# A four-layer graph attention network: the columns W a of layers l = 1 to 3 computed on TensorE from W turned

## The chip, the cores and the metric

The kernel runs on one core of a Trainium2 chip, in one launch. The time is the device time of one execution in microseconds (us); the median of three executions is compared. Engines are named as in the profile: PE is TensorE (PEld its weight loads), DVE is VectorE, ACT is ScalarE, POOL is GpSimd, SP is SyncE, which only issues DMAs here.

## The reference

The input x has 16 batch elements of 1024 nodes with 256 features, and one adjacency matrix of 1024 x 1024 serves all. Four layers follow each other; each normalises the rows of x, applies ReLU, and adds the result of a graph attention layer to x. Cut to one layer with H heads of D = 256 / H features (H is 4, 1, 4, 1 for l = 0 to 3; the slope is 0.2, 0.2, 0.2, 0.01):

```
h = max(layernorm(x), 0)
q = (h @ W).reshape(B, N, H, D)
e_src = einsum('bnhd,hd->bnh', q, a_src);  e_dst = einsum('bnhd,hd->bnh', q, a_dst)
e = leaky_relu(e_src[:, :, None, :] + e_dst[:, None, :, :], slope)
attn = softmax(where(mask, e, -inf), axis=2)
x = x + act(einsum('bijh,bjhd->bihd', attn, q))        # elu, relu in the last layer
```

Layer 0 has one pair of vectors a for all heads, layer 2 one pair for each head, layers 1 and 3 have one head. Since e_src = h (W a_src), the kernel appends W a_src and W a_dst to W as extra columns and gets the scores out of the projection itself. How these columns of W a are computed is what the change touches; it is done once per layer, for all batch elements.

## The kernel before, in words

Four batch elements (streams) are under way at once. The order of the 64 steps (one step is one layer of one batch element) is fixed by `order_of_steps`: streams 0, 1, 2, 0, 3, 1, 2, and so on. The program is written in the order in which each engine is to work; semaphores are put in by the framework, and a tile of a pool with n buffers waits until the one n allocations ago has been read for the last time.

*A step.* The preparation of a step (lines 231 to 376) takes the statistics of the rows on DVE (`stats`, L243), combines them on POOL or DVE, normalises on ACT (L290), turns the rows (by TensorE, L321, in the first two steps and the last; else by ACT L299, a transposing DMA L301 and ACT L307), projects on TensorE (`project`, L332, with W and its appended columns in `wx[l]`) and copies the result with ACT (L334). From the appended columns come the factors `rcol` (L340) and `gcol` (L350, L351); `gcol` is turned into rows (L358, L360), written to DRAM (`grow`, L362) and fetched back, spread over all partitions (`gs`, L386), and ACT copies it to PSUM as `g` (L397). For each head and each of the eight blocks of nodes, DVE makes one tile of attention weights `w` (L411, one instruction on 128 x 1024), and TensorE multiplies it with the projected rows (`aggregate`, L428); ACT copies the sums to `y` (L443). `finish` divides, applies the activation and adds to x on DVE, ACT and POOL.

*Order.* A step has eight groups of aggregation. After group k of step n the loop at lines 673 to 696 runs, in this order: pieces of the finish of the step before, one piece out of the dictionary `later` if position 8 n + k has one (L690), the pieces of coming preparations that are due at this position (`prepare`), and new `w` tiles (`emit_tiles`). `w` has WBUFS = 18 buffers, also used for other tiles of that name; PSUM has four buffers named `bank`.

*The columns.* `weight_columns(l)` gives four pieces: `vectors` fetches the two vectors (2 KB) into partition 0 of a `w` tile (L145, one DMA), `spread` copies them to all partitions with one matmul against ones (L152) and ACT (L155), `columns` multiplies W with them on DVE and sums each head (L162 and L163, four times each) and squares (L169), `bound` sums the squares over the partitions on TensorE (L175), takes the maximum on DVE (L178) and makes three bias values on POOL (L179 to L182). For l = 0 this runs at the very beginning. For l = 1, 2, 3 the pieces stand at positions 1, 27 and 43 of `later` and 1, 2 and 8 positions after (L670).

At the start SP issues, in this order: x of stream 0, W of l = 0, the eight blocks of the adjacency matrix, x of stream 1, W of l = 1, x of streams 2 and 3 (L631 to L638). W of l = 2 and 3 follows at L668.

Of the kernel before, what the change touches and what calls it, by code (L numbers as in the profile page):

```python
# [26 lines left out]
F32 = mybir.dt.float32  # L27
# [4 lines left out]
AF = mybir.ActivationFunctionType  # L32
ALU = mybir.AluOpType
# [3 lines left out]
P = 128  # L37
# [3 lines left out]
WBUFS = 18  # L41
# [29 lines left out]
def kernel(ctx: ExitStack, tc: tile.TileContext, x, adj, ws, avs, out):  # L71
    nc = tc.nc
    B, N, F = x.shape
    C = N // P
    K = F // P
    HALF = C // 2

    const = ctx.enter_context(tc.tile_pool(name="const", bufs=1))

    ident = const.tile([P, P], F32, name="ident")  # L80
# [10 lines left out]
    wx = []  # L91
# [12 lines left out]
    small = ctx.enter_context(tc.tile_pool(name="small", bufs=4))  # L104
    work = ctx.enter_context(tc.tile_pool(name="work", bufs=2))
# [5 lines left out]
    L = len(LAYERS)  # L111
# [4 lines left out]
    def bank(*shape):  # L116
        t = ps.tile([P, 512], F32, name="bank")
        n = math.prod(shape)
        if len(shape) == 1:
            return t[:, 0:n]  # L120
        names = "abc"[:len(shape)]
        return t[:, 0:n].rearrange(f"p ({' '.join(names)}) -> p {' '.join(names)}",
                                   **dict(zip(names, shape)))

    def heads_of(t, H):


        return t[..., 0:F + H].rearrange("p c (h d) -> p c h d", h=H)

    def load_weights(l, queue=nc.sync):  # L130
        H = LAYERS[l][0]
        for k in range(K):
            queue.dma_start(out=heads_of(wx[l], H)[:, k, :, 0:F // H],
                            in_=ws[l][k * P:(k + 1) * P, :].rearrange("p (h d) -> p h d", h=H))

    def weight_columns(l):

        H, slope, hs, _ = LAYERS[l]
        D = F // H
        st = {}  # L140

        def vectors(queue=nc.sync):

            st["a"] = work.tile([P, HALF, H, D], F32, name="w", bufs=WBUFS)
            queue.dma_start(  # L145
                out=st["a"][0:1, 2:4],
                in_=bass.AP(tensor=avs[l].tensor, offset=avs[l].offset,
                            ap=[[0, 1], [D, 2], [hs, H], [1, D]]))

        def spread():  # L150
            pa = bank(2, H, D)
            nc.tensor.matmul(pa.rearrange("p t h d -> p (t h d)"), lhsT=ones[0:1, :],  # L152
                             rhs=st["a"][0:1, 2:4].rearrange("p t h d -> p (t h d)"),
                             start=True, stop=True)
            nc.scalar.activation(st["a"][:, 0:2], pa, AF.Copy)  # L155

        def columns(ks=range(K)):
            for k in ks:
                for part in range(2):
                    prod = st["a"][:, 2 + part]  # L160
                    wk = heads_of(wx[l], H)[:, k]
                    nc.vector.tensor_mul(prod, wk[:, :, 0:D], st["a"][:, part])  # L162
                    nc.vector.tensor_reduce(  # L163
                        wk[:, :, D] if part else wx[l][:, k, F + H:F + 2 * H], prod, AX.X, ALU.add)
            if K - 1 not in ks:
                return
            st["sq"] = small.tile([P, K, H], F32, name="sq", bufs=1)
            wd = heads_of(wx[l], H)[:, :, :, D]
            nc.vector.tensor_tensor(st["sq"], wd, wd, op=ALU.mult)  # L169

        def bound():

            pn = bank(H)
            for k in range(K):
                nc.tensor.matmul(pn, lhsT=ones, rhs=st["sq"][:, k, :], start=(k == 0),  # L175
                                 stop=(k == K - 1))
            top = small.tile([P, 1], F32, name="top", bufs=1)
            nc.vector.tensor_reduce(top, pn, AX.X, ALU.max)  # L178
            nc.gpsimd.tensor_tensor(top, top, half1, op=ALU.pow)  # L179
            nc.gpsimd.tensor_scalar(cbias[l], top, 16.01, None, op0=ALU.mult)  # L180
            nc.gpsimd.tensor_scalar(nbias[l], top, -16.01 * slope, None, op0=ALU.mult)
            nc.gpsimd.tensor_scalar(rbias[l], top, -16.01 * (1.0 - slope), SHIFT,  # L182
                                    op0=ALU.mult, op1=ALU.add)

        return vectors, spread, columns, bound

    pairs = {}
# [36 lines left out]
    def load(b, parts=1):  # L224
        xs[b] = xpool.tile([P, C, F], F32, name="x")
        xb = x[b].rearrange("(p c) f -> p c f", p=P)
        for i in range(parts):
            q = slice(i * C // parts, (i + 1) * C // parts)
            nc.sync.dma_start(out=xs[b][:, q], in_=xb[:, q])
# [326 lines left out]
    def prepare(upto):  # L556

        while agenda and agenda[0][0] <= upto:
            _, n, piece, last = agenda.pop(0)
            piece()  # L560
            if last:
                done["prepared"] = n + 1
# [38 lines left out]
    for n, (b, l) in enumerate(steps):  # L601
# [6 lines left out]
        start = 8 * (n - 2)  # L608
# [5 lines left out]
        if free > start + kind[0]:  # L614
            kind = LATE
            start = max(free, agenda_of[-1][0] + 5, start - LATE[7])
        if n == len(steps) - 1:
            kind, start = LAST, 8 * (n - 1)
# [8 lines left out]
    with tc.manual_schedule():  # L627
        blocks = [mask_rows(c) for c in range(C)]
        layer = [weight_columns(l) for l in range(L)]
        layer[0][0](nc.scalar)  # L630
        load(0, 2)  # L631
        load_weights(0)
        for c in range(C):
            blocks[c][0]()
        load(1)
        load_weights(1)
        for i in range(2, STREAMS):
            load(i)  # L638
        nc.scalar.activation(warm, half1, AF.Exp)
        nc.vector.tensor_copy(identb, ident)  # L640
        layer[0][1]()
        first = [piece for _, piece in preparation(0)]

        order = (

            [first[0], first[1], first[3], lambda: layer[0][2](range(1)), first[2],
             lambda: layer[0][2](range(1, K)), first[5], first[6], first[4], layer[0][3]]

            + [blocks[c][1] for c in range(4)]
            + [first[7], first[8], blocks[0][2], blocks[4][1], blocks[5][1], blocks[0][3],  # L650
               first[9], first[10], blocks[1][2], blocks[6][1], blocks[7][1], blocks[1][3],
               first[11], first[12], blocks[2][2], blocks[0][4],
               lambda: prepare(-4), first[13], first[14], blocks[1][4], blocks[2][3],
               blocks[3][2], first[15], first[16], blocks[3][3]]

            + [first[17], blocks[4][2], first[18], first[19], lambda: emit_heads(0),
               blocks[5][2], blocks[6][2], blocks[4][3], blocks[4][4], blocks[5][3], blocks[5][4],
               blocks[6][3], blocks[7][2], blocks[2][4], blocks[3][4], blocks[7][3],
               lambda: prepare(-2), blocks[6][4], lambda: prepare(-1), blocks[7][4]])
        plan(1)  # L660
        planned = 2
        done["prepared"] = 1
        for piece in order:
            piece()
        emit_tiles(C, must=True)
        prepare(-0.5)
        for i in range(2, STREAMS):
            load_weights(i)  # L668

        for l, at in ((1, 1), (2, 8 * 3 + 3), (3, 8 * 5 + 3)):  # L670
            for i, piece in zip((0, 1, 2, 8), layer[l]):
                later[at + i] = piece
        for n in range(len(steps)):
            for k, (h, i0, per) in enumerate(groups(n)):
                while planned < len(steps) and min(
                        a[0] for a in agenda_of[planned:planned + 2]) <= 8 * n + k:
                    plan(planned)
                    planned += 1
                while ending and ending[0][0] < k:
                    ending.pop(0)[1]()  # L680
                emit_tiles(place[n, h, C - 1] + 1, must=True)
                aggregate(n, h, i0, per)
                if i0 + per == C:
                    done["free"] = place[n, h, C - 1] + 1
                while ending and ending[0][0] <= k:
                    ending.pop(0)[1]()
                upto = min(done["tiles"] + (6 if per > 1 else 3), done["free"] + WBUFS)

                emit_heads(upto - 1 + (C // 2 if per == 1 and k >= C - 2 else 0))
                if 8 * n + k in later:  # L690
                    later[8 * n + k]()
                prepare(8 * n + k)
                emit_tiles(upto)
            for _, piece in ending:
                piece()
            ending = finish(n) if n < len(steps) - 1 else []
# [35 lines left out]
```

## Time and profile before

| | us |
|---|---|
| median of 3 executions | 2452.1 |
| lowest, highest | 2447.61, 2452.8 |
| the profiled execution's own time | 2451.16 |
| span of the profiled execution (first to last instruction) | 2449.4 |
| busy: PE, DVE, ACT, POOL | 2393.3, 2048.9, 1478.8, 1069.9 |
| L428, aggregation on PE, 36864 records | 1896.7 |
| L332, projection on PE, 2048 records | 485.8 |
| L411, weight tiles on DVE, 1288 instructions | 1539.8 |
| L162, one of 16 products / L163, one of 16 reductions (median) | 0.416 / 0.420 |
| L152, one of 8 records of the spread (median) | 0.662 |
| L175, one of 16 records of the bound (median) | 0.252 |

The time is a little longer than the span, by what lies before the first and after the last instruction. Busy time of an engine is the sum over its instructions; a share of 98% says that there was nearly always one under way, not that each was needed then. The records of PE are modelled: an f32 matmul has two records and two weight loads. A row of the order of work gives start and length in us, the engine and line, output and inputs by the program's names, their sizes, and, in brackets, how long the engine stood idle before and what released it.

### The profile page before, as it was taken

To read this page: it belongs to the slowest core of one execution; us is meant where nothing else is said; L and a number is where in the kernel's file an instruction comes from. 1 tells how busy PE (TensorE), PEld (TensorE's weight loads), DVE (VectorE), ACT (ScalarE), POOL (GpSimd) and SP (SyncE) were. 2 spreads that over 40 slices of the span, in tenths; PEclk is the share of its full clock that TensorE was granted. 3 is DMA by queue.
4 is the path that set the end of the run, shared out by engine and by line. 5 is a ranking of instruction groups with operands and counts; after the bars stand their busy time and mean duration, and the time that the engine had idled before them with its cause. 6 is when DMAs were issued, how large, how long until landed. Compare 5 with 4: busy or idle time off the path is not lost.

```text
span 2449.4 us, 86561 instructions
## 1 busy us (share of the span) xinstructions
PE 2393.3 (98%) x39127; PEld 2149.5 (88%) x39127; DVE 2048.9 (84%) x2168; ACT 1478.8 (60%) x2499; POOL 1069.9 (44%) x1346
## 2 busy tenths in 40 slices
PE   7999999999999999999999999999999999999999
PEld 5888788889898899898898888899988988888897
DVE  8988688988888988888988888888888888888794
ACT  5465676556665656765656765666665567656542
POOL 3345455543345454544333554543443445544331
PEclk9999999999999999999999999999999999999999
DMA  4322232233333322333433323223323323323320
GB/s 181 81 54 62 44 79 62 71 103 91 97 77 90 80 63 46 79 71 96 114 92 85 79 62 71 71 54 97 97 80 105 97 46 79 71 62 77 73 54 35
DMA packets 290442, 191.84 MB, mean 78 GB/s; under 512 B 259998, under 2 KB 262806, under 8 KB 288152
## 3 DMA queue, kind: packets, MB, share of 16 engines
q1 hardware_dynamic: 290062, 186.29, 30.0%
q8 instruction: 307, 5.03, 0.8%
q14 instruction: 63, 0.52, 0.1%
q10 hardware_dynamic: 10, 0.00, 0.0%
HBM read 104.87 MB, written 17.43 MB: 50 GB/s over the span
## 4 chain that ended last, share of the span: by engine, by line
PE 80%; ACT 7%; DVE 6%; DMA 5%; issue 2%; POOL 0%; SPq 0%; DVEq 0%; ACTq 0%
PE bank L428 62%; PE bank L332 17%; DVE w L411 4%; DMA gs<-grow 2%; ACT rows L290 2%; DMA grow<-gT 2%; ACT rows L299 1%; ACT g L397 1%; ACT rows L481 1%; DVE bn L243 1%; ACT y L443 1%; ACT rows L307 0%; DMA rows<-rows 0%; DVE rows L487 0%; PE bank L358 0%
## 5 line engine op out<-in xcount | busy, mean ns | idle before, releaser
L428 PE MATMUL bank<-whx,w 128*64 128x65 f32 x36864 | 1896.7, 240 | 18.7 <-DVE w L411 9.8
L428 PEld LDWEIGHTS bank<-whx,w 128*64 128x64 f32 x36864 | 1745.6, 144 | 176.2 <-issue 21.7
L411 DVE SCALAR_TENSOR_TENSOR w<-g,rcol,mask 128x1024 f32<-128x1024 f32 (+1 forms) x1288 | 1539.8, 1268 | 195.9 <-PE bank L428 161.1
L344 POOL TENSOR_TENSOR whx<-whx 128x1024 f32<-128x1024 f32 x128 | 244.6, 1911 | 845.8 <-ACT whx L342 845.8
L443 ACT ACTIVATE y<-bank 128x260 f32<-128x260 f32 (+1 forms) x504 | 191.9, 381 | 560.3 <-PE bank L428 560.2
L332 PE MATMUL bank<-wx,rows 128*128 128x264 f32 (+1 forms) x2048 | 485.8, 391 | 14.7 <-ACT y L443 8.8
L332 PEld LDWEIGHTS bank<-wx,rows 128*128 128x128 f32 x2048 | 381.5, 191 | 90.3 <-ACT y L443 14.8
L475 POOL TENSOR_TENSOR y<-y,r 128x1024 f32<-128x1024 f32 x124 | 257.6, 2086 | 224.6 <-DVE rows L474 188.8
L334 ACT ACTIVATE whx<-bank 128x264 f32<-128x264 f32 (+1 forms) x512 | 194.1, 388 | 190.6 <-PE bank L332 190.3
L290 ACT ACTIVATE rows<-x,shift,rstd 128x256 f32<-128x256 f32 x512 | 264.5, 588 | 66.6 <-POOL shift L284 61.4
L488 POOL TENSOR_TENSOR x<-x,rows 128x1024 f32<-128x1024 f32 x94 | 222.3, 2365 | 178.4 <-DVE rows L487 178.4
L307 ACT ACTIVATE rows<-rows 128x2048 uint16<-128x2048 uint16 x122 | 261.7, 2145 | 20.6 <-DMA rows<-rows 20.6
L299 ACT ACTIVATE rows<-rows 128x2048 uint16<-128x2048 uint16 x122 | 233.1, 1911 | 3.9
L487 DVE SCALAR_TENSOR_TENSOR rows<-rows,y 128x1024 f32<-128x1024 f32 x94 | 186.0, 1979 | 45.2 <-ACT rows L481 39.7
L243 DVE BATCH_NORM_STATS2 bn<-x 128x6 f32<-128x256 f32 x512 | 175.7, 410 | 34.3 <-POOL x L488 31.1
L397 ACT ACTIVATE g<-gs 128x1024 f32<-128x1024 f32 x158 | 161.7, 1023 | 66.7 <-DMA gs<-grow 54.0
L278 POOL TENSOR_TENSOR rstd<-rstd,neghalf 128x4 f32<-128x4 f32 (+1 forms) x97 | 121.2, 1249 | 41.0 <-DVE shift L279 33.8
L481 ACT ACTIVATE rows<-rows 128x1024 f32<-128x1024 f32 x96 | 100.6, 1048 | 9.9 <-DVE rows L510 7.9
L464 DVE RECIPROCAL r<-y 128x32 f32<-128x32 f32 (+1 forms) x63 | 17.3, 275 | 98.5 <-ACT y L443 98.5
L474 DVE SCALAR_TENSOR_TENSOR rows<-y,r 128x1024 f32<-128x1024 f32 x58 | 68.5, 1222 | 1.1
L342 ACT ACTIVATE whx<-whx,nbias 128x16 f32<-128x16 f32 (+1 forms) x128 | 40.2, 314 | 4.2
L340 ACT ACTIVATE rcol<-whx,rbias 128x16 f32<-128x16 f32 (+1 forms) x128 | 39.9, 312 | 4.2
(73 smaller groups left out, 463.7 us busy)
## 6 DMA issues: line engine op xcount, KB each, us to landing
gs<-grow SPq DMA_DIRECT2D x158, 512.0 KB
x<-in_x SPq DMA_DIRECT2D x15, 1024.0 KB
out<-x SPq DMA_DIRECT2D x30, 512.0 KB
w<-in_adj SPq DMA_DIRECT2D x8, 512.0 KB
rows<-rows SPq DMA_TRANSPOSE x122
x<-in_x SPq DMA_DIRECT2D x2, 512.0 KB
wx<-in_L_gnn_W SPq DMA_DIRECT2D x8, 128.0 KB
out<-x SPq DMA_DIRECT2D x8, 128.0 KB
```

The costliest lines, as they stand in the source:

```text
L243: nc.vector.bn_stats(bn[:, c, :], xs[b][:, c, :])
L290: nc.scalar.activation(xn[:, :, q, :], xs[b][:, c, :].rearrange("p (k i) -> p k i", k=K), AF.Relu, bias=st["shift"][:, c:c + 1], scale=st[ ...
L299: nc.scalar.activation(bits, xn.rearrange("p (n s) -> p s n", s=2), AF.Copy)
L307: nc.scalar.activation(st["hT", half].rearrange("p k i -> p (k i)").bitcast(U16).rearrange("p (n s) -> p n s", s=2), st["turned", half].re ...
L332: nc.tensor.matmul(pw, lhsT=st["hT", half][:, k, q * P:(q + 1) * P], rhs=wx[l][:, k, :], start=(k == 0), stop=(k == K - 1))
L334: nc.scalar.activation(st["whx"][:, c, :], pw, AF.Copy)
L344: nc.gpsimd.tensor_tensor(wh[:, :, :, 0:D], wh[:, :, :, 0:D], wh[:, :, :, D:D + 1].to_broadcast([P, HALF, H, D]), op=ALU.mult)
L411: nc.vector.scalar_tensor_tensor(state[n]["w", h, j][:, s], state[n]["g", h][:, s], state[n]["rcol"][:, j, h:h + 1], masks[LAYERS[steps[n] ...
L428: nc.tensor.matmul(acc[o % P:o % P + cols, q, :], lhsT=st["w", h, jc][:, o:o + cols], rhs=st["whx"][:, jc, h * (D + 1):(h + 1) * (D + 1)], ...
L443: nc.scalar.activation(st["y"][:, i0:i0 + per, h, :], acc, AF.Copy)
L475: nc.gpsimd.tensor_tensor(yh, yh, rb, op=ALU.mult)
L488: nc.gpsimd.tensor_add(xh, xh, e)
```

## The change

For l = 1, 2 and 3, `weight_columns` returns four other pieces. `vectors_down` fetches the vectors of a layer from DRAM one element per partition, into a tile of their own with one column for each head and part; elements of other heads are zero (filled by POOL, where H > 1). These are 4, 8 and 4 DMAs, all issued by SP at the beginning, after the loads of x. `turned` multiplies W with the identity on TensorE, so that W transposed stands in one PSUM bank, and ACT copies it to a `w` tile. `products` multiplies W transposed with the vectors on TensorE, ACT copies the two sets of columns into `wx[l]`, and POOL squares one of them. `bound` is as before. `turned` stands where `spread` stood, `products` where `columns` stood and `bound` where it stood; nothing stands at the position of the fetch. Layer 0 keeps the old pieces.

```diff
+        def vectors_down():
+            a = st["a"] = const.tile([P, K, 2 * H], F32, name=f"down{l}")
+            if H > 1:
+                nc.gpsimd.memset(a, 0.0)
+            for part, column in ((1, 0), (0, H)):
+                for h in range(H):
+                    for k in range(K):
+                        if h * D // P <= k <= ((h + 1) * D - 1) // P:
+                            lo = max(h * D, k * P)
+                            size = min((h + 1) * D, (k + 1) * P) - lo
+                            nc.sync.dma_start(
+                                out=a[lo - k * P:lo - k * P + size, k, column + h:column + h + 1],
+                                in_=bass.AP(tensor=avs[l].tensor,
+                                            offset=avs[l].offset + h * hs + part * D + lo - h * D,
+                                            ap=[[1, size], [1, 1]]))
+
+        def turned():
+            pt = bank(K, K, P)
+            for k in range(K):
+                wk = heads_of(wx[l], H)[:, k, :, 0:D]
+                size = min(D, P)
+                for lo in range(0, F, size):
+                    h, d = divmod(lo, D)
+                    nc.tensor.matmul(pt[lo % P:lo % P + size, lo // P, k, :],
+                                     lhsT=wk[:, h, d:d + size], rhs=ident, start=True, stop=True)
+            st["wT"] = work.tile([P, K, K, P], F32, name="w", bufs=WBUFS)
+            nc.scalar.activation(st["wT"], pt, AF.Copy)
+
+        def products():
+            pw = bank(K, 2 * H)
+            for k in range(K):
+                for d in range(K):
+                    nc.tensor.matmul(pw[:, k, :], lhsT=st["wT"][:, d, k, :], rhs=st["a"][:, d, :],
+                                     start=(d == 0), stop=(d == K - 1))
+            wd = heads_of(wx[l], H)[:, :, :, D]
+            nc.scalar.activation(wd, pw[:, :, 0:H], AF.Copy)
+            nc.scalar.activation(wx[l][:, :, F + H:F + 2 * H], pw[:, :, H:2 * H], AF.Copy)
+            st["sq"] = small.tile([P, K, H], F32, name="sq", bufs=1)
+            nc.gpsimd.tensor_tensor(st["sq"], wd, wd, op=ALU.mult)
+
+        if l > 0:
+            return vectors_down, turned, products, bound
         return vectors, spread, columns, bound
...
         for i in range(2, STREAMS):
             load(i)
+        for l in range(1, L):
+            layer[l][0]()
         nc.scalar.activation(warm, half1, AF.Exp)
...
-        for l, at in ((1, 1), (2, 8 * 3 + 3), (3, 8 * 5 + 3)):
-            for i, piece in zip((0, 1, 2, 8), layer[l]):
+        for l, at in ((1, 2), (2, 8 * 3 + 4), (3, 8 * 5 + 4)):
+            for i, piece in zip((0, 1, 7), layer[l][1:]):
                 later[at + i] = piece
```

## The prediction

> **What bounds the kernel now.** I read the page's busy shares and chain first, then busy time by stretches of 20 us (one start of each of the three replaced computations lies at 62, 203 and 285 us), then TensorE's and VectorE's order of work around these places, and last the queue of SyncE at the start. The page:
>
> ```profile
> PE 2393.3 (98%) x39127; PEld 2149.5 (88%) x39127; DVE 2048.9 (84%) x2168; ACT 1478.8 (60%) x2499; POOL 1069.9 (44%) x1346
> ...
> PE 80%; ACT 7%; DVE 6%; DMA 5%; issue 2%; POOL 0%; SPq 0%; DVEq 0%; ACTq 0%
> ```
>
> Over the whole, TensorE sets the time. The change touches only the first 320 us, so that stretch has to be read by itself. Columns: stretch, length, then busy us (instructions) of PE, weight loads, DVE, ACT, POOL, the granted clock and DMA:
>
> ```profile
> 60.00:80.00 20.00, 19.02 (x483) 16.78 (x479) 19.83 (x24) 14.38 (x22) 1.51 (x1) 1.00 0.66 135
> 100.00:120.00 20.00, 18.02 (x569) 17.27 (x564) 20.00 (x25) 6.01 (x9) 12.30 (x13) 1.00 0.26 83
> 120.00:140.00 20.00, 14.66 (x368) 13.64 (x368) 20.00 (x24) 11.98 (x15) 8.72 (x28) 0.83 0.35 71
> 200.00:220.00 20.00, 19.18 (x147) 15.81 (x147) 19.83 (x25) 15.61 (x24) 5.19 (x15) 1.00 0.38 80
> 280.00:300.00 20.00, 18.84 (x84) 15.32 (x83) 9.65 (x14) 12.30 (x22) 4.13 (x3) 1.00 0.21 54
> ```
>
> Up to 140 us VectorE is full and TensorE has holes: the first step waits for weight tiles (L411). From 160 us TensorE is full. So l=1's columns stand in a VectorE-bound stretch, those of l=2 and l=3 in TensorE-bound ones. The order of work, first of VectorE, then of TensorE, shows it (start, us, engine, line; in brackets the idle time before and its releaser):
>
> ```profile
> 70.13 0.41 DVE L162 TENSOR_TENSOR w<-wx,w 128x256 f32<-128x256 f32 x1
> ...
> 73.39 0.16 DVE L169 TENSOR_TENSOR sq<-wx 128x2 f32<-128x2 f32 x1
> 73.47 26.30 DVE L411 SCALAR_TENSOR_TENSOR w<-g,rcol,mask 128x1024 f32<-128x1024 f32 x22
> ```
>
> ```profile
> 121.70 0.34 PE L428 MATMUL bank<-whx,w 128*64 128x65 f32 x4 [0.86 <-DVE w L411]
> ...
> 202.74 1.09 PE L152 MATMUL bank<-w,ones 1*128 1x512 f32 x2 [0.82 <-DMA w<-in_L_gnn_a]
> 203.76 10.69 PE L428 MATMUL bank<-whx,w 128*128 128x257 f32 x48
> ...
> 236.78 0.61 PE L175 MATMUL bank<-sq,ones 128*128 128x4 f32 x4
> 237.25 0.27 PE L358 MATMUL bank<-ident,gcol 128*8 128x128 f32 x1
> ...
> 285.32 1.09 PE L152 MATMUL bank<-w,ones 1*128 1x512 f32 x2 [1.16 <-DMA w<-in_L_gnn_a]
> 286.34 3.74 PE L428 MATMUL bank<-whx,w 128*128 128x257 f32 x16
> ```
>
> The reader sees l=1's columns hold VectorE from 70.13 to 73.47, and TensorE twice standing still until a vector's fetch has landed.
>
> [...] The trace's four L175 loads take 0.52 us, 130 ns each[...]. [...] the trace shows no gap where L332's 128 columns give way to L428's 64 (214.29 plus 3.65 against 217.87), so I charge nothing. [...]
>
> **The change part by part.** *Removed, VectorE:* per layer four products (0.41), four reductions (0.42) and a square (0.16), 3.5 us busy. For l=1 that is 73.47 - 70.13 = 3.34 us of a full engine that TensorE is waiting for at 110 to 136 us (waits like the 0.86 above; TensorE's waits on L411 in its first 330 us sum to 9.8 us, some 6.5 of them here, the rest at 246 to 250). I take 3.3 us off the path; bounds 0 and 3.5. For l=2 it is 209.00 to 212.34, but VectorE then waits 5.39 us, until 228.62, for TensorE to release a weight tile: the saving lengthens this wait, gain 0. For l=3 VectorE has just waited 12 us for g, gain 0.
>
> *Removed, TensorE:* the spread of the vectors, with its wait: l=1 62.20 to 63.25, 1.05 us; l=2 from 201.91 (L428 ends, 187.85 + 14.06) to 203.76, 1.85; l=3 from 284.16 (280.52 + 3.64) to 286.34, 2.18.
>
> *Added, TensorE:* an f32 matmul has two records. Turning W for l=1 and l=3: four of 128 by 128, eight records. By columns, L428's 257 take 14.06 / 64 = 0.22 us, so 128 take 0.11; a load takes 0.13. At 0.13: 1.04 us. For l=2: eight of 64 columns, sixteen records; L428's 65 moving columns take 11.42 / 384 = 0.030, both halves overlapping, so 128 take 0.059: 0.94 us (without overlap 0.11 each, 1.76). Products: four matmuls of 2 or 8 columns, like L175: four records hold TensorE from 236.78 to 237.25, 0.47, and another time 0.36; eight take 0.83. The lower bound of a record is 0.09, the upper L175's median of 0.252, as if nothing were hidden. Net: l=1 1.04 + 0.83 - 1.05 = +0.82, hidden in TensorE's waits for VectorE at 105 to 138 us (on the path +0.82 if they were gone); l=2 0.94 + 0.83 - 1.85 = -0.08; l=3 1.87 - 2.18 = -0.31.
>
> *ScalarE:* the copy of W turned takes the place of the copy of the vectors (0.59, same size); two small copies are new, 0.3 each like L342. They stand behind y (L443) of the same group. For l=1 the merge L307 at 69.94 moves by 0.6, and L332 behind it, which TensorE waits for at 72.13. TensorE is then 0.8 late itself, and gets it back at 85.17, where it waits 1.25 for a merge behind L397, which waited 2.25 for VectorE. Path 0, at most +0.6 per layer. *POOL:* the square moves there, some 0.2 us (L272 on 128x4); POOL then idles 21.65 us before L344. Its reader, the bound's matmul, comes six groups later. *Buffers:* one w tile is taken as before. Counting lines 681 to 693, 14 of 18 are held at l=2 and 8 at l=3, so the copy finds its tile free. One bank more is taken per layer; of four, the one of four uses ago is long copied.
>
> *Moved:* three fetches leave SyncE's queue at 45.7, 200 and 283.6 us; sixteen (4 for l=1, 8 for l=2, 4 for l=3) come at the start, between these two:
>
> ```profile
> 12.56 1.62 SPq L229 DMA_DIRECT2D x<-in_x  x2
> 31.86 0.78 SPq L362 DMA_DIRECT2D grow<-gT  x1
> ```
>
> SyncE is idle from 14.2 to 31.86. The x load at 8.73 waited for a mask fetch eight issues before it, so I take eight to be in flight at most: seven of the sixteen go out by about 24 us, the eighth waits for the last x, whose data end at 26.06 in the trace, and eight follow it. Issues here took 0.26 to 0.78 us; at 0.4 they end at 29.7, before grow's issue. The data are nothing: the 4-byte packets that the trace has take 9 ns. With 0.78, grow is 1.2 us late; its rows land by 38.5 and L397 takes them at 41.80, so 3.3 us are spare. Cost 0, upper end about 2 us if the issues are as slow as the 1.25 us that ACT's took. The fill of the zeros on POOL (0.1 us) comes at 1.5, SyncE waits for it before 14.2: nothing.
>
> **Sum.** -3.3 - 0.08 - 0.31 = -3.7 us against the profiled execution's 2451.16 (span 2449.4): 2447.5. By the same share, 0.15%, the median of 2452.1 becomes 2448.4. Later stretches only shift, being full on TensorE.
>
> **Rivals.**
> *A: VectorE's saving doesn't reach the end.* It turns into waits for g copies or for the merges, since ScalarE is busy 17.37 of 20 us at 140 to 160 and releases TensorE at 140.50. For it: the bound's maximum (L178) would be reached at 101.6, just when its matmul ends, and may stand 0.8. Against: the merge at 140 follows statistics on VectorE at 123.96, with it full until then, so it moves along. Then 2452.1 - 0.4 = 2451.7.
> *B: l=2 gains too.* TensorE waits some 3.3 us for VectorE at 246 to 250. If VectorE's lead counted there, -7.0: 2445.1. Against: the wait of 5.39 at 228.62 takes up all of it.
> *C, slower: TensorE's records are not hidden.* If weight loads of such small matmuls stand alone at 0.252 us, l=2's 24 records take 6.05 and l=3's 16 take 4.03: +4.2 and +1.85, less 3.3: +2.8, 2454.9. It decides from 0.18 us a record, where 40 records cost 7.3 = 1.85 + 2.18 + 3.3. For it: L332's loads average 0.186. Against: those overlap longer matmuls, and L175's spacing is 0.09 to 0.12.
> *D: the fetches delay the start,* up to +2 less 3.7: 2450.4.
>
> **How the numbers follow.** 0.2% of this kernel, 4.9 us, is about what a measurement can tell from no change. Forecast 0.52, A 0.2, B 0.1, C 0.12, D 0.06. The runs of before spread over 5 us, so each case is smeared by some 2.5 us. The forecast falls below 2447.2 in about 3 of 10 and B in 8 of 10, with a few of A and D: faster 0.26. Slower needs 2457.0, C's upper part: 0.07. Range 2443.5 to 2456, from B's lower side to C's upper; the forecast's own is 2445 to 2452.
>
> **What would show it.** Right: VectorE goes from w to w at 70 us; l=1's first step ends about 3.3 us earlier by 158 us (now 157.95 starts a run of L428), with shorter PE waits on L411; turning plus products take 1.8 us per layer on TensorE; waits on the vectors are gone. Wrong: a product record above 0.18 us, a TensorE wait for the copy of W turned, grow issued after 33 us, or the lead at 158 us lost by 330.

## The result and the profile after

Median of 20 runs each on the same chips: 2446.28 us (2443.45 to 2452.53) after, 2451.95 us (2447.61 to 2459.83) before. The ratio is 0.9979, 95% interval 0.9972 to 0.9987: 5.1 us faster, between 3.2 and 6.9. The forecast was 3.7 us faster. The profiled execution took 2449.74 us, its span is 2448.0 us. One execution of an experiment below (layer 1 alone) took 2717.79 us at a granted clock of 0.849 where the others had 0.99 to 1.00; it is in no figure here.

The page of the changed kernel, busy shares:

```profile
PE 2394.8 (98%) x39177; PEld 2153.2 (88%) x39177; DVE 2040.0 (83%) x2141; ACT 1480.0 (60%) x2505; POOL 1073.7 (44%) x1350
```

DVE lost 27 instructions and 8.9 us of busy time, PE gained 50 records and 1.5 us. Four of the stretches of 20 us that were shown of before (stretch, length, busy us of PE, weight loads, DVE, ACT, POOL, clock, DMA):

```profile
60.00:80.00 20.00, 19.94 (x491) 18.29 (x488) 20.00 (x17) 15.58 (x26) 0.52 (x2) 1.00 0.64 142
...
120.00:140.00 20.00, 16.41 (x372) 15.15 (x372) 20.00 (x23) 13.77 (x19) 5.74 (x20) 0.91 0.46 81
...
200.00:220.00 20.00, 20.00 (x206) 17.47 (x205) 15.84 (x15) 15.36 (x25) 5.80 (x8) 1.00 0.29 54
280.00:300.00 20.00, 20.00 (x100) 17.52 (x99) 9.83 (x9) 9.80 (x23) 4.12 (x4) 1.00 0.10 31
```

DVE is still full to 140 us: the first step stays bound by it, only with fewer instructions. PE is full at 200 and 280 us, where it had holes of 0.82 and 1.16 us for the vectors' fetches. The order of work of DVE (l=1's place, then l=2's), and of PE (l=1, the end of the first step, l=2):

```profile
53.82 41.80 DVE L455 SCALAR_TENSOR_TENSOR w<-g,rcol,mask 128x1024 f32<-128x1024 f32 x35
...
207.52 3.67 DVE L455 SCALAR_TENSOR_TENSOR w<-g,rcol,mask 128x1024 f32<-128x1024 f32 x3 [1.38 <-PE bank L472]
...
224.69 6.05 DVE L455 SCALAR_TENSOR_TENSOR w<-g,rcol,mask 128x1024 f32<-128x1024 f32 x5 [7.47 <-PE bank L472]
```

```profile
61.01 1.16 PE L210 MATMUL bank<-ident,wx 128*128 128x128 f32 x8
62.01 0.27 PE L402 MATMUL bank<-ident,gcol 128*32 128x128 f32 x1
...
66.09 1.05 PE L219 MATMUL bank<-down,w 128*128 128x2 f32 x8
67.07 1.15 PE L472 MATMUL bank<-whx,w 128*64 128x65 f32 x31
...
153.75 11.42 PE L472 MATMUL bank<-whx,w 128*64 128x65 f32 x384
...
197.71 1.09 PE L210 MATMUL bank<-ident,wx 128*64 128x128 f32 x16
198.74 3.74 PE L472 MATMUL bank<-whx,w 128*128 128x257 f32 x16
202.41 1.06 PE L219 MATMUL bank<-down,w 128*128 128x8 f32 x8
203.33 7.20 PE L472 MATMUL bank<-whx,w 128*128 128x257 f32 x32
```

DVE goes from `w` to `w` through 70 us. The run of 384 records, which began at 157.88, begins at 153.75. From start to next start, turning takes 1.00 and 1.03 us, the products 0.98 and 0.92, with no wait before any of them. For l=2 DVE's wait was 5.39 us; now it waits 1.38 and 7.47: the time saved there became waiting. The two rows of before, of PE and of DVE:

```profile
157.88 11.42 PE L428 MATMUL bank<-whx,w 128*64 128x65 f32 x384
```

```profile
228.62 7.24 DVE L411 SCALAR_TENSOR_TENSOR w<-g,rcol,mask 128x1024 f32<-128x1024 f32 x6 [5.39 <-PE bank L428]
```

PE's waits from 50 to 142 us, before and then after (for what, us in total, times, longest):

```profile
PE bank L428 <- DVE w L411: 6.5, 8, 0.9
PE bank L332 <- ACT rows L307: 3.3, 3, 1.2
```

```profile
PE bank L472 <- DVE w L455: 5.8, 8, 0.9
PE bank L376 <- ACT rows L351: 1.1, 1, 1.1
```

They fall by 2.9 us, but those for weight tiles only by 0.7 (by 3.7 and 1.7 against the second execution of before, below). The rest is PE's waits for merges. The one of 0.98 us at 72.13 is filled by PE's own new work. The one of 1.25 at 85.17 is gone: ACT no longer stands still for DVE at the copy of `g` ahead of that merge, which starts at 80.04 us and not at 82.98. The copy, before and after:

```profile
80.74 1.03 ACT L397 ACTIVATE g<-gs 128x1024 f32<-128x1024 f32 x1 [2.25 <-DVE w L411]
```

```profile
77.34 1.02 ACT L441 ACTIVATE g<-gs 128x1024 f32<-128x1024 f32 x1
```

SyncE's queue at the start (start, length, line, transfers):

```profile
15.05 17.75 SPq L197 DMA_DIRECT2D down<-in_L_gnn_a  x16
32.91 0.77 SPq L406 DMA_DIRECT2D grow<-gT  x1
```

What SyncE waited for from 14.9 to 32.9 us (for what, us in total, times, longest):

```profile
SPq L197 <- DMA x<-in_x: 6.7, 3, 3.0
SPq L197 <- DMA w<-in_adj: 2.7, 3, 1.0
```

The sixteen fetches hold SyncE until 32.80 us, 9.4 us of it waiting for earlier loads, and `grow` goes out 1.05 us later than before.

### The profile page after: what moved, and what is told of

It reads as the page before. It is cut to its first block, busy times and chain, and to the rows that moved or that the text cites. A ratio compares the mean times of both kernels' runs of the same rounds, so it can differ in the third digit from the quotient of the medians.

```text
span 2448.0 us, 86681 instructions
## 1 busy us (share of the span) xinstructions
PE 2394.8 (98%) x39177; PEld 2153.2 (88%) x39177; DVE 2040.0 (83%) x2141; ACT 1480.0 (60%) x2505; POOL 1073.7 (44%) x1350
## 4 chain that ended last, share of the span: by engine, by line
PE 82%; ACT 7%; DMA 5%; DVE 4%; issue 2%; POOL 0%; SPq 0%; DVEq 0%; ACTq 0%
PE bank L472 64%; PE bank L376 17%; DVE w L455 2%; DMA gs<-grow 2%; ACT rows L334 2%; DMA grow<-gT 2%; ACT g L441 1%; ACT rows L343 1%; ACT rows L525 1%; ACT rows L351 1%; ACT y L487 1%; DVE bn L287 1%; DMA rows<-rows 0%; PE bank L402 0%; ACT whx L378 0%
## 5 line engine op out<-in xcount | busy, mean ns | idle before, releaser
L351 ACT ACTIVATE rows<-rows 128x2048 uint16<-128x2048 uint16 x122 | 261.6, 2144 | 22.7 <-DMA rows<-rows 22.6
```

What stands on the lines that cost most here:

```text
L351: nc.scalar.activation(st["hT", half].rearrange("p k i -> p (k i)").bitcast(U16).rearrange("p (n s) -> p n s", s=2), st["turned", half].re ...
```

## The experiments

Besides the time I use marks: the start of the i-th copy of sums to `y` by ACT (L443 of before), the same piece of work in every kernel. The table gives, at the time that a mark has in the profile of before, how many us later (+) or earlier a kernel reaches it, in one execution each.

| mark at | 50 | 140 | 188 | 256 | 330 | 828 | 1711 | 2393 |
|---|---|---|---|---|---|---|---|---|
| before, again | -1.1 | -0.7 | -0.8 | -1.2 | -0.9 | -1.0 | -2.8 | -4.6 |
| after | -1.2 | -4.1 | -4.1 | -4.6 | -4.8 | -3.5 | +3.4 | -1.5 |
| l=1 only | -1.3 | -4.3 | -4.3 | -4.6 | -4.7 | -2.9 | -0.1 | -4.0 |
| l=2, 3 only | -1.6 | -1.2 | -1.2 | -1.7 | -2.2 | +0.7 | +6.6 | +1.2 |
| DVE work back, l=1 | -1.3 | -0.5 | -0.5 | -1.0 | -1.7 | -1.7 | +5.1 | +1.8 |
| DVE work back, l=2, 3 | -0.5 | -2.0 | -2.2 | -2.6 | -2.2 | -3.0 | +0.7 | +1.1 |
| fetches only | +0.5 | +0.9 | +0.6 | +1.8 | +1.7 | +3.3 | +1.9 | -1.5 |
| fetches twice | +7.9 | +5.2 | +7.2 | +6.7 | +6.3 | +5.1 | +1.9 | +1.1 |
| l=0 too | +4.2 | +2.7 | +4.0 | +3.5 | +3.7 | -0.5 | -8.5 | -14.3 |
| after, 64 bytes | +0.3 | -3.1 | -3.1 | -3.0 | -3.7 | -7.7 | -11.6 | -18.2 |
| after, 64 bytes behind x | -1.0 | -4.0 | -4.0 | -4.4 | -4.8 | -8.6 | -13.8 | -20.9 |
| before, 192 bytes | -0.5 | -0.4 | -0.4 | -0.3 | -0.3 | -5.1 | -12.7 | -20.9 |

**The kernel before, once more.** No edit.

> The kernel before once more, for its order of work alone. The changed kernel and three of four experiments were 1.2 to 1.6 us ahead of the profile of before already when the first copy of sums to y starts (49.8 us there), before any new work of TensorE. If that is the spread of the start from one execution to the next, this profile has the first copy anywhere between 48.2 and 49.8 us; if the 16 fetches or what goes with them speed the start, it is at 49.6 to 50 again. Between the first copy and 330 us I expect the same as before within 0.5 us, and after that a drift of some us either way.

2446.62 us in its one run, span 2444.8. At the marks to 330 us the two executions keep their distance within 0.5 us; by the end they are 4.6 apart. So marks up to about 330 us can show a fraction of a microsecond where several executions agree, and later ones only several. One execution alone is no proof: that of the fetches alone, whose work from 50 to 330 us is the same as before, moves by 1.3 us there.

**Layer 1 alone, layers 2 and 3 alone.**

```diff
-        if l > 0:
+        if l in (1,):
             return vectors_down, turned, products, bound
```

(and the fetches and positions to match; `(2, 3)` in the other kernel)

> Layers 2 and 3 keep the old pieces, only layer 1 gets its columns from TensorE. My theory (the gain is the 3.3 us that VectorE no longer spends while TensorE waits for it): -3 to -4 us against before, and the first run of 384 aggregation records after 150 us starts at 154 to 155 us (157.9 before, 153.8 in the changed kernel). Rival (the gain is the two fetch waits and spreads that leave TensorE in layers 2 and 3): within 1 us of before, and that run starts near 157.

> Layer 1 keeps the old pieces, layers 2 and 3 get their columns from TensorE. My theory: -0.4 to -1 us against before; the first run of 384 aggregation records after 150 us starts at 157 to 158 us as before, and the distance from it to the same aggregation group near 330 us shrinks by 0.4 to 1 us. Rival (layers 2 and 3 hold the gain): -4 to -5 us.

Layer 1 alone: 2447.76 us, ratio 0.9987 (0.9979 to 0.9995), some 3 us faster. Layers 2 and 3 alone: 2449.80 us, 0.9993 (0.9979 to 1.0006), which could be nothing. The marks place it. From 50 to 140 us, against the second execution of before, the full change and layer 1 alone gain 3.3 us each and the others alone 0.0 (against the first execution, 2.9 and 3.0). The run of 384 records begins at 153.62 us with layer 1 alone and at 156.65 with layers 2 and 3 alone, each some 0.4 us before the range expected of it; both executions were already 1.3 and 1.6 us ahead at the first mark. From 188 to 256 us (l=2) the full change gains 0.4 us and so does the unchanged kernel run again. From 256 to 308 us (l=3) the full change and layers 2 and 3 alone both gain 0.5 us; layer 1 alone and the repeat gain less than 0.1.

**DVE's work put back beside the new pieces.** If the change works by what DVE no longer does, it must vanish when DVE does as much again.

```diff
         def products():
+            if l in (1,):
+                extra = st["both"][:, 1]
+                for k in range(K):
+                    for part in range(2):
+                        w0 = wx[0][:, k, 0:F].rearrange("p (h d) -> p h d", h=H)
+                        prod = extra[:, 0:F].rearrange("p (h d) -> p h d", h=H)
+                        nc.vector.tensor_mul(prod, w0, w0)
+                        nc.vector.tensor_reduce(extra[:, F:F + H], prod, AX.X, ALU.add)
+                nc.vector.tensor_tensor(extra[:, 0:H], extra[:, F:F + H], extra[:, F:F + H], op=ALU.mult)
             pw = bank(K, 2 * H)
```

(`(2, 3)` in the other kernel; `st["both"]` is the `w` tile that holds W turned, and the half of it written here is read by nothing)

> The changed kernel, with nine VectorE operations of the old sizes (four products, four reductions, a square, into scratch memory that nothing reads) put back where layer 1's columns stood. My theory: nearly all of the gain goes, -0.5 to -2 us against before, and TensorE waits for weight tiles between 100 and 140 us as long as before (6.5 us in waits that the profile names). Rival (the gain comes from the fetches or from TensorE's side): still -4 to -5 us.

> The changed kernel, with the nine VectorE operations put back where the columns of layers 2 and 3 stood, not in layer 1. My theory: no difference from the changed kernel, -4 to -6 us against before, since VectorE waits 7.5 us for a free weight tile shortly after layer 2's place and for g before layer 3's. Rival (VectorE's time counts there too): 3 to 7 us slower than the changed kernel, about like before.

For l=1: 2449.61 us, 0.9992 (0.9980 to 1.0004), not told from before. The lead is gone: ACT's wait ahead of the merge is back, 2.89 us, PE's waits for weight tiles from 100 to 140 us are 7.5 us (6.5 before), and the run of 384 records begins at 157.38, close to 157.88 of before:

```profile
157.38 11.42 PE L482 MATMUL bank<-whx,w 128*64 128x65 f32 x384
```

For l=2 and 3: 2445.97 us, 0.9975 (0.9967 to 0.9983), as fast as the full change. VectorE's order there shows why:

```profile
206.84 0.41 DVE L223 TENSOR_TENSOR w<-wx 128x256 f32<-128x256 f32 x1
...
226.62 6.05 DVE L465 SCALAR_TENSOR_TENSOR w<-g,rcol,mask 128x1024 f32<-128x1024 f32 x5 [5.16 <-PE bank L482]
```

With 3.7 us of work back, the wait for a weight buffer is 5.16 us, where it was 7.47 and 1.38 without: the wait absorbs it. These two kernels and the changed one have their tiles at the same addresses, which will matter below; of the two, the one with the work back in layer 1 is 3.6 us slower by medians. One thing is not clean: in the execution with l=2 and 3 the lead shrank by 1.6 us between 115 and 140 us, where its program is that of the changed kernel; the median of its 22 runs does not show it. The granted clock from 130 to 140 us was 0.66 in it and 1.00 in the changed kernel's, but that this was the cause is not shown.

**The fetches alone, and the fetches twice.**

```diff
+        for l in range(1, L):
+            layer[l][0](True)
```

(in the changed kernel, into tiles that nothing reads; the other run adds the sixteen fetches to the kernel before)

> The kernel before, with the 16 fetches added at the start into memory that nothing reads, all else old. My theory: no difference, within 1 us of before; grow is issued at 32 to 33.5 us, the first copy of sums to y starts between 48.2 and 49.8 us. Rival (the fetches help the start): -1 to -1.5 us. Rival (the fetches delay the start): +1 to +2 us.

> The changed kernel with all 16 fetches issued twice, the second time into memory that nothing reads. From the spacing of the sixteen (17.75 us from the first to the end of the last, 6.7 us of it waiting for the last loads of x) I expect the second sixteen to take 7 to 10 us and grow to be issued at 40 to 43 us instead of 32.9, so that the copy of the second head's rows to PSUM begins at 46 to 49 us instead of 41.0. My theory of slack (3.3 us before ScalarE waits, some 9 before VectorE does): ScalarE 5 to 8 us late there, VectorE 0 to 2 us; -1 to -5 us against before. Rival (the start has no slack for the fetches): 5 to 8 us slower than the changed kernel.

Alone: 2451.68 us, 1.0008 (0.9998 to 1.0018) of before: between 0.5 us faster and 4.4 slower, not told from nothing; it has its tiles at other addresses than before, too. `grow` goes out at 32.73, and the first copy of sums half a microsecond later than the range expected. Twice: 2451.43 us, 1.0010 (1.0001 to 1.0019), so the whole gain is lost and more: by the ratios this is 7.6 us slower than the changed kernel, and the rival came true. Its queue:

```profile
33.23 1.85 SPq L199 DMA_DIRECT2D down1True<-in_L_gnn_a  x4
35.19 4.95 SPq L199 DMA_DIRECT2D down2True<-in_L_gnn_a  x8
40.18 2.01 SPq L199 DMA_DIRECT2D down3True<-in_L_gnn_a  x4
42.29 0.77 SPq L408 DMA_DIRECT2D grow<-gT  x1
```

With no load of x ahead, the second sixteen take 1.85, 4.95 and 2.01 us, about 0.55 each. `grow` is 9.4 us later than in the changed kernel (10.4 than before), and the mark at 50 us is 9.1 us later than in the changed kernel, 7.9 and 9.0 later than in the two executions of before. So before had some 1.3 to 2.5 us to spare there, and the changed kernel next to nothing.

**Layer 0 too.** Layer 0's columns move to TensorE as well, its eight fetches issued by ScalarE.

```diff
-        if l > 0:
-            return vectors_down, turned, products, bound
-        return vectors, spread, columns, bound
+        return vectors_down, turned, products, bound
```

(and `nc.scalar` as the queue of these fetches, and the pieces of layer 0 put into the opening order)

> The changed kernel with layer 0 in the new way as well: its eight fetches issued by ScalarE at the very start, W turned before the first statistics, the products after the first transposes, the bound after the first projection. VectorE's chain at the start holds 3.5 us of layer 0's columns (10.0 to 13.7 us) and 1.1 us of waiting for the bound. My theory: the first weight tile of attention on VectorE starts 1 to 3 us earlier, and the kernel is 1 to 3 us faster than the changed one. Rival (the projection, behind W turned, its copy and the products, is not earlier, or the matrix's loads set the start): no difference from the changed kernel, or up to 1 us slower.

2437.02 us, 0.9949 (0.9935 to 0.9962), and not by its own work. Against both expectations it reaches the mark at 50 us 4.2 us late. ScalarE's fetches take 10.52 us, and the eight adjacency blocks take SyncE 10.22 us to issue instead of 4.90, with 2.4 us of waiting for these fetches and 4.1 for one of the blocks. It wins 18 us between 330 us and the end, where its program is that of the changed kernel. What differs there: the 256-byte packets, nearly all of them those of the transposing DMAs (122 of 512 KB), take 21.1 ns on average, against 23.8 to 24.7 in the others so far. And its new tile of 64 bytes puts the tiles `rows`, from and into which these DMAs go, at byte 76032 of a partition in the built program, a multiple of 256; in before and after they begin at 75840 and 75968, which leave 64 and 192. That became the next theory.

**64 bytes of padding.**

```diff
     warm = const.tile([P, 1], F32, name="warm")
+    nc.gpsimd.memset(const.tile([P, 16], F32, name="pad"), 0.0)
```

(in the changed kernel; 48 elements instead of 16 in the kernel before, the same 16 in the kernel with layer 0 too, and in the last one in a pool between those of x and of `rows`)

> The changed kernel with one unused tile of 64 bytes per partition (filled once by GpSimd), so that every later tile begins 64 bytes further on: the tiles rows, source of the transposing DMAs, then begin at byte 76032 of a partition, a multiple of 256, instead of 75968. Theory (the run with layer 0's columns on TensorE too owes its gain to where its tiles lie): the transposing DMA's packets take about 21 ns instead of 24, TensorE's waits for y between 400 and 2350 us fall from 8 to 11 us to below 3, and the time is 2432 to 2440, 9 to 14 us below the changed kernel's 2446.3 and 12 to 20 below the kernel before. Rival (that run gained by what it does in layer 0, by its late start or by the other order of its loads): no change against the changed kernel, 2445 to 2448, packets at 24 ns.

> The kernel before with one unused tile of 192 bytes per partition (filled once by GpSimd), so that its tiles lie at the same addresses as those of the changed kernel with 64 bytes more (rows at 76032). Theory (addresses): 2436 to 2443, 9 to 15 us below the kernel before, with packets of about 21 ns; and the changed kernel with 64 bytes stays 3 to 5 us below this one, which is the change at equal addresses. Rival (addresses do nothing): 2450 to 2454, the same as the kernel before. If addresses also made part of the change's own gain, the two padded kernels lie within 2 us of each other.

> The kernel with layer 0's columns on TensorE too, and 64 bytes per partition of unused tile, so that its rows begin at 76096, which is 64 past a multiple of 128, as in the changed kernel. Theory (addresses): its gain is lost, and with its start later by some 5 us it takes 2450 to 2456, 13 to 19 us more than without the 64 bytes; packets at 24 ns. Rival (its gain comes from its own work, not from addresses): 2435 to 2439 as before, packets at 21 ns.

> The changed kernel with the 64 unused bytes placed between the tiles of x and the tiles rows: x stays where it is in the changed kernel (64 past a multiple of 128), while rows and all tiles behind them lie as in the kernel with 64 bytes at the front. If the place of rows or of what lies behind them decides: the same time as that kernel within 2 us, 2432 to 2440, and packets of 21 ns. If the place of x or of the constants decides: no gain, 2445 to 2448, packets of 24 ns. If addresses do nothing: 2445 to 2448 in both.

| | rows begin at, remainder by 256 | 256-byte packet, mean ns | us | ratio to before (2447.52) |
|---|---|---|---|---|
| after, 64 bytes | 76032, 0 | 21.0 | 2430.65 | 0.9927 (0.9914 to 0.9939) |
| before, 192 bytes | 76032, 0 | 21.0 | 2433.16 | 0.9940 (0.9928 to 0.9952) |
| l=0 too, 64 bytes | 76096, 64 | 23.8 | 2453.56 | 1.0026 (1.0015 to 1.0038) |
| after, 64 bytes behind x | 76032, 0 | 21.3 | 2429.34 | 0.9921 (0.9909 to 0.9934) |

Three of the four came out 1 to 3 us below the ranges expected of them, and the changed kernel with 64 bytes waits 5.2 us for `y` where less than 3 was expected. An unused tile makes the kernel before 14.4 us faster, and 64 bytes more take the gain from the kernel with layer 0 too: it is the place of the tiles. The place of x made no difference (2430.65 and 2429.34). The last run does not part `rows` from the tiles behind it, which moved along; but among them the transposing DMAs' packets are what the trace shows changed. The page's line of the DMA queue (packets, MB, share of 16 engines) for the kernel before, then with 192 bytes:

```profile
q1 hardware_dynamic: 290062, 186.29, 30.0%
```

```profile
q1 hardware_dynamic: 290062, 186.29, 28.1%
```

PE's largest waits of the same two from 330 to 2350 us (for what, us in total, times, longest; "issue" is waiting for nothing that the profile shows):

```profile
PE bank L332 <- ACT y L443: 8.1, 11, 1.5
PE bank L428 <- issue: 7.4, 13, 1.2
```

```profile
PE bank L333 <- ACT y L444: 2.2, 5, 1.0
```

The mean hides what happens to a packet. In every one of the fourteen profiles the median of the 256-byte packets is 18 ns. Where `rows` begins at a multiple of 256, 1.5 to 1.6% of them took longer than 18 ns; at the remainders 64, 96 (layer 1 alone) and 160 (layers 2 and 3 alone) it was 20.0 to 20.5%, at 192 22.0 to 22.7%. So a fifth of the packets grew, most of them to between 19 and 52 ns, and the rest not at all. In sum over the 251,912 packets of these two profiles it is 722 us, 45 us on each of 16 engines, which is most of the drop from 30.0 to 28.1%.

ScalarE's wait for these DMAs before the merge falls from 20.6 to 10.2 us, and its wait for `gs` ahead of the copy of `g` from 48.2 to 43.0 (400 to 2350 us). In the kernel before, ScalarE comes to each of the eleven `y` that TensorE waits for straight from a copy of `g` that had waited 1.40 to 4.13 us for `gs`; in eight of the eleven, the merge before that copy had waited 0.82 to 1.99 us for its DMA. In one of them the merge at 880.68 had waited 1.42 us and the copy of `g` at 884.72 1.89; `y` is copied at 885.68, and TensorE projects at 886.10, after 0.67 us of waiting. Whether the transposing DMAs' packets delay `gs`, and how, is not shown. All of TensorE's waits there fall from 17.6 us (14.9 in the repeat of before) to 3.2. Of the 17.6, 8.0 are named "issue"; they are gone too, but what ends them is not shown. These two executions' spans are 20.9 us apart: 14.4 us of waits, and 6.4 us of PE's busy time (2393.3 and 2386.9; 2390.2 in the repeat), which stays open.

In every run here the two go together: with `rows` at the remainders 64, 96, 160 and 192 the packets took 23.8 to 24.7 ns on average, at remainder 0 21.0 to 21.3. Why they do, and why four fifths of the packets take no longer at the other remainders, no trace shows: the effect is shown, its cause is not.

The two padded kernels have their tiles at the same addresses and differ by the change alone: 2.5 us by medians of five, 3.1 by means, in the forecast's direction and near its size, but their spread allows no change as well. Taken together, the two padded forms of the changed kernel (ten runs, `rows` at the same byte) are 3.6 us below it by means, 95% interval 1.1 to 6.2: so the change gives a few microseconds at equal addresses too. The fastest version is the changed kernel with the padding, 17 to 18 us below before.

## Why the prediction was right

- **VectorE's saving for l=1, 3.3 us on the path.** The size is right: 3.3 us by the marks from 50 to 140 us, for the full change and for layer 1 alone; put back, it costs all of that. Rival A falls. The way was in part another. The forecast took all of it from the waits for weight tiles at 110 to 136 us; but 1.5 of the 3.3 us are there by the mark at 91 us, ahead of those waits. They come from the merge at 85.17, whose wait the forecast had kept, to make up for ScalarE's delay. TensorE's +0.82 for l=1 was hidden in the merge wait at 72.13, not in those at 105 to 138.
- **l=2's saving absorbed by the wait of 5.39 us.** Right: the wait grew to 7.47 and 1.38, and putting the work back costs nothing. Rival B falls, though the median alone (2446.28) lies nearer to its 2445.1 than to the forecast's 2448.4.
- **TensorE's terms.** Turning and products take 1.98, 1.95 and, from the same view at 279.63 and 284.00, 1.70 us for the three layers, where 1.87, 1.77 and 1.87 were worked out. With what was removed, l=3's net is -0.48, put at -0.31, and l=2's is +0.10, put at -0.08. A record takes 0.06 to 0.13 us from start to start (0.064 in the sixteen of 64 columns, 0.125 in l=1's eight of 128), never the 0.18 from which rival C decides.
- **The sum.** At 330 us the changed kernel is 3.8 us ahead of the second execution of before and 4.8 of the first; -3.7 was forecast. The timed 5.1 us has -3.7 in its interval; the 1.4 between is not explained and can't be told from spread.
- **SyncE's sixteen fetches** is the step that was mis-sized. At 0.4 us each they were to end at 29.7, with `grow` on time; they ended at 32.80. Seven were out by 24.6, as worked out, and the next waited for x: that fits the forecast's estimate of eight in flight, drawn from the load at 8.73. But the other nine took 8.2 us to 32.80, not 5.1 to 29.7, since an issue takes 0.52 us on average without the waits (17.75 less 9.4, over 16) and there are three waits for x, not one. So `grow` was 1.05 us late. The cost of 0 survived because that is within the slack; yet the slack was some 1.3 to 2.5 us, not 3.3, as the doubled fetches show. Rival D was closer to coming true than its chance of 0.06 says.
- **What no step had.** The forecast counted only the first 320 us as touched. But the change adds tiles to a pool that lies ahead of `rows`. 128 bytes moved them from remainder 64 to 192, and both are slow (packets of 23.9 and 24.7 ns). 64 bytes more would have moved the time by some 13 us (0.9979 against 0.9927), more than twice what the change gave. That it came out right here is luck.

## What to carry to other kernels

Where an engine's work is removed, ask of each place separately whether the engine sets the time there: the same 3.5 us of VectorE was worth some 3 us in the first step and nothing in the fourth, where a wait for a buffer took it up. Follow it over the engines between: here nearly half of it reached TensorE by way of ScalarE, which had waited for VectorE, and not through the weight tiles. The tiny fetches here cost their issue (0.52 us each on SyncE, where one of their 4-byte packets took 9 ns), and stood in a queue ahead of something. When a change adds or removes a tile, compare both kernels with the tiles of the DMAs at the same addresses, or the difference may belong to the addresses; and try multiples of 256 bytes, with which three kernels here were 13 to 19 us faster.

## What was unexpected of the hardware

- With the source and target of the transposing DMAs at a multiple of 256 bytes, their 256-byte packets took 21.0 to 21.3 ns on average, elsewhere 23.8 to 24.7 (1.5 to 1.6% above 18 ns in place of 20.0 to 22.7%), and three kernels of this study were 13 to 19 us faster, though the DMA engines were busy only 30% of the time.
- Sixteen fetches of at most 512 bytes hold SyncE 17.75 us, of which 9.4 us is waiting for earlier loads; the rest is 0.52 us each, and 0.55 in the second sixteen of the doubled run. Eight from ScalarE took 10.52 us, though one issue took 0.51 us in the median, and SyncE's eight issues beside them 10.22 us instead of 4.90, 6.5 us of it waiting.
- Two executions of one program drift apart by several us, here 4.6 by the end, after agreeing within 0.5 us over the first 330.
